# Stores on ScalarE's queue, and buffers moved from decays to rows and recalled tiles, in a hybrid attention and state-space layer

## The chip, the cores and the metric

The kernel runs on one core of a Trainium2 chip. The metric is the device time in microseconds (us) of one execution. The engines are TensorE (PE, with its weight loads PEld), VectorE (DVE), ScalarE (ACT), GpSimd (POOL) and SyncE (SP), whose queue issues DMAs.

## The reference

Four stages in a row change x, of 4 x 256 tokens with 512 features in float32: an attention, a gated feed-forward, a state-space mixer, and the feed-forward again. The change lies in the mixer. Cut to what matters:

```python
x = x + attention(layernorm(x))
x = x + ffn(layernorm(x))
x = x + mixer(layernorm(x))
x = x + ffn(layernorm(x))

def mixer(u):                       # H=128 heads of 64, G=8 groups, state 128
    gate, xBC, dt = split(u @ in_proj_w.T)
    hs, Bm, Cm = split(silu(causal_conv4(xBC) + conv_b))
    dt = softplus(dt + dt_bias); cum = cumsum(dt * A)
    # per head: y[i] = sum_{j<=i} (C_i . B_j) exp(cum_i - cum_j) dt_j x_j
    y = ssd(hs, ...) + D * hs
    g = y * silu(gate)
    g = g * rsqrt(mean(g*g over each of 8 groups) + eps) * norm_w
    return g @ out_w.T
```

The reference sums over chunks of 32 tokens and carries a state; the kernel forms the whole sum over 256 tokens per head directly, as a lower triangular matrix of decays times scores.

## The kernel before, in words

All matrix products that need float32 accuracy are made of three products of high and low parts (`mm3`, L115 to L117); `split` (L107, L108) makes the parts, the high one on ScalarE, the low one on VectorE or GpSimd.

The mixer runs over 64 blocks of 128 inner channels, 8 blocks to a group. One block i has two heads, 2i and 2i+1. It does the following:

- It projects its 128 channels of x (pp, 24 matmuls of 128x512) and convolves them: L964 on ScalarE, three taps at L971 on VectorE, SiLU at L975 on ScalarE. The result is x2, turned to token rows by trx (L1027) and scaled to xd (L1030).
- It projects the gate (again pp) and takes its SiLU, gt, on ScalarE (L1218).
- `differences` makes the decays em of each of the two heads from r, a row of cumulated values that `rows` (L996) loads from memory broadcast to all partitions. Four subtractions L1004 on VectorE, a mask L1008 on GpSimd, which overwrites half of r, then exponentials on ScalarE: four at L1013, one at L1014, four at L1016, the last readers of r.
- `weighted` (L1020) multiplies em by the scores gm of the group, on VectorE.
- `product` (L1044) multiplies em by xd on TensorE, for the block before. It is the last reader of em of both heads.
- `gated` adds the skip term (L1054), multiplies by gt (L1057) to gb, stores gb to the DRAM tile spill (L1059), squares it (L1064 for the first block of a group, L1066 for the others, which overwrites x2), and adds the squares up on GpSimd (L1067).

One group later the stored blocks come back: `recall` loads half a tile, gr (L1103), and splits it to gh; `partial` multiplies it by the output weights wo into pog, and `scaled` (L1115) adds it to x. `PER` says how many tiles of the group before are recalled in each block. In the first block of a group new scores are made. `fetch` (L811) loads the projection's weights wr, and `out_weights` (L1076) the output weights wor.

Who comes when: from block 8 on TensorE's order is that of the program text. The orders on the other engines and on SyncE's queue come from a planner that takes whatever its own estimate of time says is ready, the earlier in the text first. A queue runs its list strictly in order. `load` is `nc.sync.dma_start`, so in the mixer every transfer, loads and stores alike, stands in SyncE's one list. A tile with a tag has a number of buffers (`bufs`); a new tile waits until the oldest buffer's last reader is done. gh has three buffers, gb three, gt one.

The mixer's blocks are called in this order of steps:

```python
x2 = conv(projected("x", i, turn), i, "x2", 2)
...
inner_products(i - 1)
...
nc.scalar.activation(gt, pp, AF.Silu)
...
em.append(differences(h, rr.pop(h)))
if h + 2 < H:
    rr[h + 2] = rows(h + 2)
```

In the blocks 7, 0 and 1 of a group (from group 0's block 7 on) the inner products come between the two halves of the gate's projection, otherwise ahead of it. A row is thus always asked for two heads ahead.

Of the kernel before, what the change touches and what calls it, by code (L numbers as in the profile page):

```python
# [9 lines left out]
F32 = mybir.dt.float32  # L10
# [4 lines left out]
AF = mybir.ActivationFunctionType  # L15
# [5 lines left out]
P = 128  # L21
B, L, C = 4, 256, 512
NT = B * L
# [7 lines left out]
GB = NB // G  # L31
# [48 lines left out]
def hybrid_kernel(  # L80
# [6 lines left out]
    nc = tc.nc  # L87
    load = nc.sync.dma_start
# [16 lines left out]
    def split(hl, v, engine=nc.vector):  # L105

        nc.scalar.copy(hl[0], v)  # L107
        engine.tensor_tensor(hl[1], v, hl[0].bitcast(F32), ALU.subtract)  # L108
# [677 lines left out]
    def mixer(feed, later):  # L786
        with ExitStack() as es, ExitStack() as inner:
# [8 lines left out]
            po_ = pool("mo", 2, **freed)  # L796
# [52 lines left out]
            first = [ps_p.tile([P, NT], F32, name="pp", tag="pp") for _ in range(2)]  # L849
# [42 lines left out]
            p2 = inside("m2", 2, **freed)  # L892
# [99 lines left out]
                    yield  # L992

            def rows(h):
                r = p2.tile([P, NT], F32, name="r", tag="r", bufs=2)
                load(r, cumd[h : h + 1, :].to_broadcast([P, NT]))  # L996
                return r

            def differences(h, r):

                e = p2.tile([P, B, 3, P], F32, name="em", tag="em", bufs=4)
                rv = r.rearrange("p (b c i) -> p b c i", b=B, c=2)
                for b in range(B):
                    nc.vector.tensor_scalar(  # L1004
                        e[:, b, 2, :], rv[:, b, 1, :], col_t[:, h, b, 1:2], 0.0,
                        ALU.subtract, ALU.min,
                    )
                nc.gpsimd.affine_select(  # L1008
                    rv[:, :, 0, :], rv[:, :, 0, :], pattern=[[0, B], [1, P]],
                    compare_op=ALU.is_ge, fill=-1e30, base=0, channel_multiplier=-1,  # L1010
                )
                for b in range(B):
                    nc.scalar.activation(e[:, b, 1, :], rv[:, b, 1, :], AF.Exp, bias=col_t[:, h, b, 2:3])  # L1013
                nc.scalar.activation(e[:, :, 2, :], e[:, :, 2, :], AF.Exp)  # L1014
                for b in range(B):
                    nc.scalar.activation(e[:, b, 0, :], rv[:, b, 0, :], AF.Exp, bias=col_t[:, h, b, 0:1])  # L1016
                return e
# [33 lines left out]
            def gated(n, x2, gt, py, sq):  # L1051

                gb = po_.tile([P, NT], F32, name="gb", tag="gb", bufs=3)
                nc.vector.scalar_tensor_tensor(  # L1054
                    gb, x2, dh[:, n : n + 1], py.rearrange("p b t -> p (b t)"), ALU.mult, ALU.add
                )
                nc.vector.tensor_tensor(gb, gb, gt, ALU.mult)  # L1057
                if n < NB - 1:
                    load(spill[(n // GB) % 2][n % GB], gb)  # L1059
                else:  # L1060
                    last.append(gb)
                if sq is None:
                    sq = p2.tile([P, NT], F32, name="sq", tag="sq")
                    nc.scalar.activation(sq, gb, AF.Square)  # L1064
                else:
                    nc.scalar.activation(x2, gb, AF.Square)  # L1066
                    (nc.gpsimd if n < NB - 1 else nc.vector).tensor_tensor(sq, sq, x2, ALU.add)  # L1067
                return sq

            last = []  # L1070
            spill = [dram.tile([GB, P, NT], F32, name=f"spill{i}") for i in range(2)]
# [24 lines left out]

            def recall(g, t, half):

                r = po_.tile([P, 4, P], F32, name="gr", tag="gr", bufs=2)
                s = [po_.tile([P, 4, P], F32R, name=f"gh{j}", tag=f"gh{j}", bufs=3) for j in range(2)]  # L1100
                ts = slice(t * P, (t + 1) * P)
                n = 3 if half == 1 and g == G - 1 else 4
                load(r[:, :n, :], spill[g % 2][half * 4 : half * 4 + n, :, ts].rearrange("k p t -> p k t"))  # L1103
                split([v[:, :n, :] for v in s], r[:, :n, :])
                if n < 4:
                    split([v[:, n, :] for v in s], last[0][:, ts])
                return s
# [52 lines left out]
            def inner_products(m):  # L1160
                px2, gt, xd, em = stage.pop(m)
                py = product(xd, em)
                sqs[m // GB] = gated(m, px2, gt, py, sqs.get(m // GB))
# [5 lines left out]
            for _ in range(B):  # L1169
                next(scoring)  # L1170
            rr = {h: rows(h) for h in range(2)}
            stage, sqs, wos, rgs, todo = {}, {}, {}, {}, []
            recalled = []
            PER = {1: 1, 2: 2, 3: 1, 4: 1, 5: 2, 6: 1}
            def block(i, scoring, gm):
# [44 lines left out]
                for h in (2 * i, 2 * i + 1):  # L1220
                    with tc.issue_after(silus[2]) if i == 0 else ExitStack():
# [3 lines that stand above are left out]
# [6 lines left out]
                for _ in range(PER.get(gi + 1, 0)):  # L1231
                    if todo:
                        q, t = todo.pop(0)
                        recalled.append((q, t, [recall(q, t, half) for half in range(2)]))
# [19 lines left out]
            def begun(t):  # L1254
                pos[t] = ps_o.tile([P, C], F32, name="pog", tag="po")
                partial(pos[t], G - 1, recall(G - 1, t, 0), 0)
# [20 lines left out]
            for t in range(TT):  # L1277
                po = pos.pop(t)
                partial(po, G - 1, recall(G - 1, t, 1), 1)
                scaled(G - 1, t, po)  # L1280
                if t + 4 < TT:
                    begun(t + 4)
                feed.norm.stats(t)
                rooted = feed.norm.root(t, t + 1)

                with tc.issue_after(rooted) if t == TT - 1 else ExitStack():
                    for n in range(*{TT - 2: (0, 0), TT - 1: (t - 2, t)}.get(t, (max(0, t - 1), t))):
                        fed(n)
                xn = f2.tile([P, C], F32, name="gxn", tag="gxn")
                tr = ps.tile([P, KC, P], F32, name="tr", tag="m")  # L1290
                turned_[t] = [f2.tile([P, KC, P], F32R, name=f"gxs{j}", tag=f"gxs{j}", bufs=3) for j in range(2)]
                feed.norm.turned(t, xn, tr, turned_[t])
# [78 lines left out]
```

## Time and profile before

| | |
|---|---|
| median of 3 runs | 1880.39 us (1879.66 to 1881.84) |
| the profiled execution | 1881.98 us, its span 1880.2 us |
| attention and first feed-forward | 0 to about 408 us of the span |
| mixer's group 0, with nothing to recall | about 408 to 560 us |
| groups 1 to 7 | about 560 to 1785 us, some 180 us each |
| last recalls, second feed-forward, output | about 1785 to 1880 us |
| row load r, 512 KB at its destination, x128 | 3.9 us from issue to landing |
| store of gb, 512 KB, x63 | 3.0 us |
| recall gr, 256 KB, x120 | 3.0 us |

The span is that of the instructions from the first to the last; the execution's own time has a little around it. In the profile's busy tables each engine has its busy time in us, its share of the span, and the number of instructions. In the lists of waits each line reads: who waited, for whom, us in total, how many times, and in the queue's list the longest. The chain of waits gives start, duration and what. A busy TensorE need not be one at full speed; the pitch of its matmuls tells.

### The profile page before, as it was taken

To read this page: it belongs to the slowest core of one execution; us is meant where nothing else is said; L and a number is where in the kernel's file an instruction comes from. 1 tells how busy PE (TensorE), PEld (TensorE's weight loads), DVE (VectorE), ACT (ScalarE), POOL (GpSimd) and SP (SyncE) were. 2 spreads that over 40 slices of the span, in tenths; PEclk is the share of its full clock that TensorE was granted. 3 is DMA by queue.
4 is the path that set the end of the run, shared out by engine and by line. 5 is a ranking of instruction groups with operands and counts; after the bars stand their busy time and mean duration, and the time that the engine had idled before them with its cause. 6 is when DMAs were issued, how large, how long until landed. Compare 5 with 4: busy or idle time off the path is not lost.

```text
span 1880.2 us, 29875 instructions
## 1 busy us (share of the span) xinstructions
PE 1802.6 (96%) x10706; PEld 1449.8 (77%) x10706; DVE 1516.1 (81%) x2272; ACT 1467.9 (78%) x2886; POOL 452.0 (24%) x425
## 2 busy tenths in 40 slices
PE   8999988899999999999999999999999999999997
PEld 6777767677777887888788878877888888788876
DVE  5566667789999788977987898888888977897867
ACT  6666675379999788888888898888788978897653
POOL 6332230014441122112211311131222212321200
PEclk9999999899999999999999999999999999999999
DMA  4000000134465445544554455445535544554341
GB/s 144 1 1 1 22 15 16 34 101 157 166 199 187 133 151 164 179 140 135 196 163 140 146 176 166 143 138 184 164 128 169 184 150 131 185 175 151 101 125 50
DMA packets 152773, 240.35 MB, mean 128 GB/s; under 512 B 12464, under 2 KB 77616, under 8 KB 152624
## 3 DMA queue, kind: packets, MB, share of 16 engines
q1 hardware_dynamic: 152624, 238.44, 39.6%
q8 instruction: 84, 1.38, 0.3%
q14 instruction: 65, 0.53, 0.1%
HBM read 202.75 MB, written 35.65 MB: 127 GB/s over the span
## 4 chain that ended last, share of the span: by engine, by line
PE 59%; DVE 15%; ACT 14%; DMA 5%; issue 5%; POOL 1%; SPq 0%; ACTq 0%; DVEq 0%; POOLq 0%
PE pp L115 8%; PE pp L116 7%; PE pp L117 7%; PE pog L115 6%; PE pyy L1044 6%; PE pog L116 6%; PE pog L117 6%; DVE acc L971 4%; DVE em L1004 3%; DMA r<-cumd 3%; ACT e L477 2%; PE trx L1027 1%; ACT L1218 1%; ACT em L1016 1%; ACT em L1013 1%
## 5 line engine op out<-in xcount | busy, mean ns | idle before, releaser
L115 PE MATMUL pp<-mx,w 128*128 128x512 f32 (+1 forms) x1160 | 463.7, 400 | 13.4 <-ACT gt L1218 8.9
L117 PE MATMUL pp<-mx,w 128*128 128x512 f32 (+1 forms) x1160 | 451.8, 389 | 0.0
L116 PE MATMUL pp<-mx,w 128*128 128x512 f32 (+1 forms) x1160 | 451.7, 389 | 0.0
L971 DVE SCALAR_TENSOR_TENSOR acc<-pp,cw_s,acc 128x1012 f32<-128x1012 f32 (+2 forms) x240 | 304.8, 1270 | 56.5 <-ACT acc L964 54.5
L1020 DVE TENSOR_TENSOR em<-em,gm 128x1536 f32<-128x1536 f32 x128 | 248.1, 1948 | 39.6 <-ACT em L1016 39.5
L1008 POOL TENSOR_SCALAR_AFFINE_SELECT r<-r 128x512 f32<-128x512 f32 x128 | 121.5, 950 | 655.1 <-DMA r<-cumd 496.4
L115 PEld LDWEIGHTS pp<-mx,w 128*128 128x128 f32 x1160 | 218.4, 188 | 67.0 <-ACT gt L1218 12.4
L117 PEld LDWEIGHTS pp<-mx,w 128*128 128x128 f32 x1160 | 218.3, 188 | 46.3 <-issue 0.6
L116 PEld LDWEIGHTS pp<-mx,w 128*128 128x128 f32 x1160 | 218.6, 188 | 40.7 <-issue 0.6
L1067 POOL TENSOR_TENSOR sq<-sq,acc 128x1024 f32<-128x1024 f32 x55 | 144.7, 2632 | 334.7 <-ACT acc L1066 334.7
L1013 ACT ACTIVATE em<-r,col_t 128x128 f32<-128x128 f32 x512 | 170.0, 391 | 43.5 <-DMA r<-cumd 25.6
L115 PE MATMUL pog<-wo,gh 128*128 128x512 f32 x512 | 203.1, 397 | 0.9 <-DVE xd L1030 0.8
L1004 DVE TENSOR_SCALAR em<-r,col_t 128x128 f32<-128x128 f32 x512 | 180.3, 405 | 28.6 <-PE pyy L1044 15.0
L116 PE MATMUL pog<-wo,gh 128*128 128x512 f32 x512 | 199.6, 390 | 0.0
L117 PE MATMUL pog<-wo,gh 128*128 128x512 f32 x512 | 199.5, 390 | 0.0
L1044 PE MATMUL pyy<-em,xd 128*64 128x256 f32 (+1 forms) x2048 | 183.1, 329 | 1.3 <-DVE em L1020 0.9
L1044 PEld LDWEIGHTS pyy<-em,xd 128*64 128x64 f32 x2048 | 129.7, 137 | 59.9 <-issue 15.5
L1016 ACT ACTIVATE em<-r,col_t 128x128 f32<-128x128 f32 x512 | 167.9, 390 | 0.4
L975 ACT ACT_TABLE_LOAD x69 | 88.5, 1283 | 48.0 <-DVE acc L971 47.2
L477 ACT ACTIVATE e<-sc,nmx 128x256 f32<-128x256 f32 (+1 forms) x256 | 104.2, 442 | 21.0 <-DVE nmx L471 20.9
L108 DVE TENSOR_TENSOR gh<-gr,gh 128x512 fp32r<-128x512 f32 (+1 forms) x128 | 110.8, 874 | 7.8 <-ACT gh L107 7.3
L115 PEld LDWEIGHTS pog<-wo,gh 128*128 128x128 f32 x512 | 96.1, 188 | 26.0 <-issue 5.8
(290 smaller groups left out, 3306.9 us busy)
## 6 DMA issues: line engine op xcount, KB each, us to landing
wr<-in_win_dram SPq DMA_DIRECT2D x287, 256.0 KB, 2.7
r<-cumd SPq DMA_DIRECT2D x128, 512.0 KB, 3.9
spill<-gb SPq DMA_DIRECT2D x63, 512.0 KB, 3.0
gr<-spill SPq DMA_DIRECT2D x120, 256.0 KB, 3.0
wor<-in_wout_dram SPq DMA_DIRECT2D x64, 256.0 KB, 3.7
out_dram<-x SPq DMA_DIRECT2D x8, 256.0 KB, 2.3
x<-in_x_dram SPq DMA_DIRECT2D x1, 1536.0 KB, 8.7
gr<-spill SPq DMA_DIRECT2D x8, 192.0 KB, 2.5
```

Source lines behind the costliest of these rows:

```text
L115: nc.tensor.matmul(o, lh, rh, start=(first and k == 0), stop=False)
L116: nc.tensor.matmul(o, lh, rl, start=False, stop=False)
L117: nc.tensor.matmul(o, ll, rh, start=False, stop=(last and k == n - 1))
L477: nc.scalar.activation(es_[c][:, 2 * j + pr, :], sc[:, j, :], AF.Exp, bias=nm[:, j : j + 1], accum_out=rs[:, c, h : h + 1],)
L971: nc.vector.scalar_tensor_tensor(av[:, :, d:], pv[:, :, : L - d], cw_s[:, ch, tap : tap + 1], av[:, :, d:], ALU.mult, ALU.add,)
L1004: nc.vector.tensor_scalar(e[:, b, 2, :], rv[:, b, 1, :], col_t[:, h, b, 1:2], 0.0, ALU.subtract, ALU.min,)
L1008: nc.gpsimd.affine_select(rv[:, :, 0, :], rv[:, :, 0, :], pattern=[[0, B], [1, P]], compare_op=ALU.is_ge, fill=-1e30, base=0, channel_mult ...
L1013: nc.scalar.activation(e[:, b, 1, :], rv[:, b, 1, :], AF.Exp, bias=col_t[:, h, b, 2:3])
L1016: nc.scalar.activation(e[:, b, 0, :], rv[:, b, 0, :], AF.Exp, bias=col_t[:, h, b, 0:1])
L1020: nc.vector.tensor_tensor(e, e, gm, ALU.mult)
L1044: nc.tensor.matmul(py[d, b, k * P :], xd[:, 2 * b + k, d], es2[hh][:, b, 2 * k : 2 if k == 0 else 3, :].rearrange("p s i -> p (s i)"), sta ...
L1067: (nc.gpsimd if n < NB - 1 else nc.vector).tensor_tensor(sq, sq, x2, ALU.add)
```

## The change

The number of buffers of r and of gr goes from two to three, that of em from four to three. The store of a block is issued from ScalarE's queue in place of SyncE's, and stands behind the Square of the same block in the text. The Square itself and the sum of squares are the same as before, written in another order.

```diff
             def rows(h):
-                r = p2.tile([P, NT], F32, name="r", tag="r", bufs=2)
+                r = p2.tile([P, NT], F32, name="r", tag="r", bufs=3)
...
             def differences(h, r):
-                e = p2.tile([P, B, 3, P], F32, name="em", tag="em", bufs=4)
+                e = p2.tile([P, B, 3, P], F32, name="em", tag="em", bufs=3)
...
                 nc.vector.tensor_tensor(gb, gb, gt, ALU.mult)
+                first = sq is None
+                if first:
+                    sq = p2.tile([P, NT], F32, name="sq", tag="sq")
+                nc.scalar.activation(sq if first else x2, gb, AF.Square)
                 if n < NB - 1:
-                    load(spill[(n // GB) % 2][n % GB], gb)
+                    nc.scalar.dma_start(spill[(n // GB) % 2][n % GB], gb)
                 else:
                     last.append(gb)
-                if sq is None:
-                    sq = p2.tile([P, NT], F32, name="sq", tag="sq")
-                    nc.scalar.activation(sq, gb, AF.Square)
-                else:
-                    nc.scalar.activation(x2, gb, AF.Square)
+                if not first:
                     (nc.gpsimd if n < NB - 1 else nc.vector).tensor_tensor(sq, sq, x2, ALU.add)
...
             def recall(g, t, half):
-                r = po_.tile([P, 4, P], F32, name="gr", tag="gr", bufs=2)
+                r = po_.tile([P, 4, P], F32, name="gr", tag="gr", bufs=3)
```

## The prediction

> **What bounds the kernel now.** I read five views in this order: the busy table, the busy time by stage, TensorE's own waits, the chain of waits inside one group, and the waits of SyncE's DMA queue. The busy table and two stages (columns: start:end, length, then PE, PEld, DVE, ACT, POOL busy, each with its count):
>
> ```profile
> PE 1802.6 (96%) x10706; PEld 1449.8 (77%) x10706; DVE 1516.1 (81%) x2272; ACT 1467.9 (78%) x2886; POOL 452.0 (24%) x425
> ...
> 408.00:560.00 152.00, 145.26 (x822) 113.91 (x822) 142.39 (x177) 141.27 (x253) 64.77 (x42) 1.00 0.52 172
> ...
> 1060.00:1240.00 180.00, 177.90 (x978) 143.20 (x977) 153.06 (x194) 151.76 (x257) 38.48 (x27) 1.00 0.49 158
> ```
>
> See two regimes. In group 0 of the mixer (408 to 560 us) TensorE, VectorE and ScalarE are all above 92%. In groups 1 to 7 TensorE has 177.9 of 180 us. Busy matmuls could hide stretching, so I checked their pitch in the timeline: the 128x512 products start 0.227 us apart, for long stretches without a break. TensorE is the bound there, and all that can be won is its waits. Between 560 and 1785 us they are:
>
> ```profile
> PE pp L115 <- ACT gt L1218: 8.3, 5, 1.7
> PE trx L1027 <- ACT acc L975: 4.7, 5, 1.7
> PE pog L115 <- DVE xd L1030: 0.8, 1, 0.8
> PE pp L115 <- DVE acc L971: 0.7, 2, 0.4
> ```
>
> That is 14.5 us; 13.0 of it is ScalarE being late, once in a group. The chain of waits shows why (start, length, what):
>
> ```profile
> 1087.57 2.40 DMA wr<-in_win_dram
> 1089.98 0.33 SPq L811
> 1090.40 5.11 DMA r<-cumd
> 1095.90 0.68 ACT em L1013 x2
> 1096.60 1.28 ACT L975
> ...
> 1103.44 1.03 ACT gt L1218
> 1104.52 0.50 PE pp L115
> ```
>
> The row load of head 66 goes out at 1090.40, behind a weight fetch on SyncE; ScalarE stands still 4.3 us for it (exponentials, L1013), then runs the SiLUs late, and TensorE waits until gt at 1104.5. Such a load cannot be earlier, since its buffer is that of head 64, whose last reader (L1016) ends at 1088.5. SyncE's queue shows what else holds loads:
>
> ```profile
> SPq L1103 <- DVE gh L108: 191.4, 67, 8.3
> ...
> SPq L996 <- ACT em L1016: 160.2, 72, 5.2
> ...
> SPq L1059 <- DVE gb L1057: 113.3, 40, 11.7
> ```
>
> L1103 waits for a buffer of gr, L996 for one of r, L1059 for the block it is to store. One queue in order: behind each of them stand weight, row and recall loads.
>
> **What the Trainium skill says.** (1) "DMA: Bandwidth & Descriptors", section "Issuing engines are not separate DMA queues": issuing from several engines saves only the issuer's time, since all run on the same 16 engines. The trace agrees in size: a store costs SyncE 0.33 us and lands after 3.0. (2) "Advanced Engine Details and Errata", section "Sequencer Loop": compute instructions are queued ahead and the sequencer works on a control instruction meanwhile. So an issue on ScalarE can lie under the 1.05 us Square in front of it. Nothing in this trace shows it, ScalarE issues no DMA before. (3) "ScalarE: Activation LUTs", section "What ACT_TABLE_LOAD costs": 1283 ns for each change of set plus a drain of about 1380. The trace agrees on the 1283, and shows no drain: gt starts 1.29 us after its load does. (4) "Perfetto Trace Analysis", section "Optimization Strategy": the same gap repeating on the engine that should be full can mean too few buffers. It agrees: the gap before gt, up to 1.7 us by the waits, returns in five groups.
>
> **The change part by part.**
>
> Memory: per partition r gains 4 KB (1024 x 4 bytes), gr 2 KB, em loses 6 KB (4 x 3 x 128 x 4). Sum zero, nothing else has to move.
>
> *Rows, third buffer.* The load of head h needs the buffer of h-3 in place of h-2. For head 66 that is head 63, done with at 1074.7 in place of 1088.5: 13.8 us earlier, while the late landing cost 4.3. It covers that with 9 us to spare even if the fetch stays in front. I credit the two ScalarE waits of TensorE, 8.3 + 4.7 = **13.0 us**. Ends: nothing, if another wait takes the place (below), and 14.5 + 6.7 (TensorE idle in 408 to 560) + 2.1 (its wait for trx at 1786) = 23.3. GpSimd's 496 us wait for r is worth nothing: it is at 24%.
>
> *Recalled tiles, third buffer.* ScalarE's wait for gr's landing is 1.1 us in all; the 44.0 us it waits in front of gh (L107) are for TensorE to free gh, which keeps three buffers. The 191.4 us are SyncE's. Nothing by itself, covered by recalls running a block ahead. The 128 recall issues are the same in number; they and weight fetches may go earlier into DMA engines that are 50% busy. Between -2 and +2 us; I take 0.
>
> *The store.* Removed from SyncE: 63 issues x 0.33 = 20.8 us and waits of 113.3 us for gb, none on TensorE's path by the waits above. Added to ScalarE: the same 63 issues. It waits only for gb, which Square needs too (the DRAM slot is from two groups back), so behind it no new wait stands; queued after it are exponentials, SiLUs and casts. From below 0 (all under the Square's 1.05 us), from above 63 x 0.33 = 20.8 us of ScalarE. In groups 1 to 7 ScalarE is idle 28 of 180 us, which covers 8 x 0.33 = 2.6 per group; in group 0 it is at 93%, so I charge **2.6 us** there. The Squares (56 of 1.05, 8 of 1.04) keep their number. A block leaves some 1.1 us later if the store really goes behind the Square; gb has three buffers, and products start at least 13 us apart, so that is free.
>
> *Decays, one buffer fewer.* em for head h needs the buffer of h-3 in place of h-4. A block i uses heads 2i and 2i+1, and both go free when its product (L1044) ends. Even heads are not touched: 2i+4 waits for product i both ways, since 2i and 2i+1 are of one block. Odd head 2i+3 now waits for product i, not i-1. So from the end of product i to the start of product i+1 a whole odd head must be made: four L1004, nine exponentials (3.2 us on ScalarE plus a table load of 1.28), L1020 of 1.75. In the timeline of one group, odd heads start 22.5 to 4.1 us ahead of product i, so all shift. The room is 22.8 us in most blocks, but 14.7 before the product of block 6 of a group and 13.4 before that of block 7. Even heads do such a chain now, starting when the product ends: head 62 from 1057.9 to 1067.0, 9.1 us; head 58 from 1006.6 to 1026.9, 20.3. If odd heads take the first places after a product, 9.1 fits into 13.4, covered by matmuls; I charge 0 in groups 1 to 7. In group 0 there is less room: for blocks 0 to 7 the odd head starts ahead of the product by 1.5, 8.1, 0.8, 3.4, 3.8, 2.7, 1.1, 5.7 us, and its L1020 ends ahead of the next product by -2.7, -4.3, 2.9, 3.4, 5.0, 1.2, 7.4, -0.7. Lead beyond positive slack is 1.5 in block 5; in 0, 1 and 7 the head ends late because ScalarE is full, so a later start need not move its end. I charge **1.5 us**; upper end 1.5 + 8.1 + 1.5 + 5.7 = 16.8.
>
> Sum: -13.0 + 2.6 + 1.5 = -8.9 us. The profiled execution took 1881.98 us (span 1880.2 and 1.8 around it), 1.6 above the median 1880.39. So 1873.1 for such an execution, and **1871.5** for the median.
>
> **Rivals.**
>
> *No change: the odd head takes the place of the row wait.* At 1091.5, when product 31 ends, head 65 now comes due as well, with 3.2 us of exponentials, where ScalarE stood 4.3. Then SiLU and gt are only about 1.1 us earlier and most of the 13.0 stays: a quarter (3.3) less 2.6 gives 1879.7. For it: the same place in each group. Against: SiLU comes earlier in the block's order, and its input is ready at 1092.8.
>
> *Slower: odd heads miss their product.* Place: products of block 7 in a group, with 13.4 us of room. It decides when the chain of an odd head takes more than that; between 9.1 and 20.3 the middle is 14.7, that is 1.3 x 7 groups = 9 us, and group 0's 16.8 beside it. With the rows' gain kept and the store charged: -13.0 + 2.6 + 9 + 16.8 = +15.4, 1896; without the gain 1909. For it: TensorE has no other work in its fixed order, and ScalarE is busy nearly throughout 1060 to 1091. Against: these heads rank ahead of the next block's work.
>
> *It doesn't do what it says.* Orders on ScalarE, VectorE and SyncE come from a planner; new buffers can reshuffle them, and with them the table loads (52 for gt alone, 1.28 us each). One pair more per block is 64 x 2.6 = 164 us of ScalarE against some 200 idle in groups 1 to 7; that would show as SiLUs late everywhere. It goes either way and widens both cases.
>
> **How the numbers follow.** Forecast 0.48, no change 0.18, slower rival 0.34. A measurement can tell about 0.2%, 3.8 us. Half of reshuffling falls with the first and third. Faster 0.51 (forecast, and 0.03 of no change), within 0.2% 0.15, slower 0.34. The range goes from 1855 (the 23.3 us end, 1857, and 2 for spread) to 1902, between the 1896 and 1909 of the slower rival: left out are some 0.03 below and 0.15 above.
>
> **What would show it.** Right: ScalarE's wait for r (25.6 us) near zero, TensorE's waits for gt and acc below 4 us, stores on ScalarE with Squares unchanged, SyncE's wait at L1059 gone, and TensorE's wait for em (now about 1 us) still small. Wrong: TensorE waiting for L1020 before the product of a group's block 7 or in group 0, more than 240 table loads on the mixer's exponentials and SiLUs, or pp still waiting for gt.

## The result, and the profile after

| | median | runs |
|---|---|---|
| before, beside the changed kernel | 1884.54 us | 11 |
| the changed kernel | 1887.98 us | 11 |

The ratio is 1.0020, 95% interval 1.0008 to 1.0032: 2 to 6 us slower, where 8.9 us faster was forecast. The three runs of before shown ahead lie below the medians that later runs of it gave (1883.3 to 1884.8 us, single runs from 1875 to 1890), so a kernel is judged by its ratio to before's runs beside it. The profiled execution of the changed kernel has a span of 1887.9 us. In it the gate's SiLU has moved to L1219, the Square to L1061, the store to L1064, the recall to L1104.

The busy table and the two stages shown of before:

```profile
PE 1814.7 (96%) x10706; PEld 1459.8 (77%) x10706; DVE 1470.2 (78%) x2272; ACT 1456.8 (77%) x2876; POOL 465.8 (25%) x425
...
408.00:560.00 152.00, 144.78 (x805) 112.27 (x804) 130.79 (x166) 138.75 (x253) 62.28 (x41) 1.00 0.53 172
1060.00:1240.00 180.00, 178.75 (x983) 144.17 (x980) 146.44 (x194) 148.66 (x254) 39.31 (x27) 1.00 0.50 158
```

In a middle group TensorE is now busy 178.75 of 180 us, before 177.90: better. Group 0 has 144.78 of 152, before 145.26: no gain there. TensorE's waits from 560 to 1785 us, all that the answer has:

```profile
PE pg L986 <- DVE gm L991: 8.6, 7, 1.4
PE pyy L1044 <- DVE em L1020: 0.3, 1, 0.3
```

The waits for gt and for the SiLU of x2, 13.0 us, are gone, as forecast. A new one has come, once in a group as well: the scores' matmuls (pg) wait for VectorE to empty the earlier ones (gm). The chain of waits at the place shown of before:

```profile
1094.79 1.27 DVE acc L971
...
1096.64 1.27 DVE acc L971
1097.91 0.47 DVE gm L991
1098.43 0.70 PE pg L986 x2
```

No row load stands in it. VectorE comes late to the convolution's taps, and gm after them: measured from the start of product 31 (1091.4, before 1088.7), the first tap starts 1.6 us behind it (1093.0), before 0.6 ahead (1088.1), since ScalarE starts the convolution (L964) 0.4 ahead of it (1091.0), before 2.2 (1086.5). SyncE's queue answers to its lines of before:

```profile
SPq L1104 <- DVE gh L108: 241.8, 87, 7.5
SPq L996 <- ACT em L1016: 237.4, 76, 8.1
```

The wait for gb has left it, but the waits for buffers of gr and r have grown (191.4 and 160.2 before): loads are issued earlier, and then wait for the next buffer.

To see where the time went I divide each profiled span at the first matmul of a product (L1044) in the timeline: group 0 goes from the third masked copy of x (at 365 to 370 us in all profiles) to product 8, groups 1 to 7 on to product 63, the end from there. Table loads (`ACT_TABLE_LOAD`, 1.28 us each, which stand where ScalarE changes between exponentials and SiLUs) are counted beside them.

| profiled execution | group 0, us | its loads | groups 1 to 7, us | end, us | loads from product 8 to the last product's end | of these from product 56 on |
|---|---|---|---|---|---|---|
| before | 197.7 | 30 | 1225.9 | 90.1 | 219 | 22 |
| changed | 201.8 | 32 | 1220.5 | 96.6 | 207 | 28 |
| buffers alone (e2) | 195.0 | 26 | 1225.9 | 91.7 | 202 | 22 |
| em 3 alone (e3) | 202.8 | 32 | 1226.3 | 91.8 | 202 | 22 |
| store alone (e1) | 204.4 | 30 | 1233.6 | 90.1 | 226 | 25 |

The changed kernel loses 4.1 us in group 0 and 6.5 at the end, and wins 5.4 between. Of the 6.5, 2.2 us are a wait for em inside the last product, and 3.4 are two stretches in which TensorE ran at half its clock (last section). Single profiles spread: the same stretch of before's program (e9 below has its order on TensorE) differs by 4 us in groups 1 to 7, so sums of a few us are taken from the timed ratios, and the stretches say where.

### The profile page after: what moved, and what is told of

It is laid out like the page before. It is cut to its first block, busy times and chain, and to the rows that moved or that the text cites. A ratio compares the mean times of both kernels' runs of the same rounds, so it can differ in the third digit from the quotient of the medians.

```text
span 1887.9 us, 29843 instructions
## 1 busy us (share of the span) xinstructions
PE 1814.7 (96%) x10706; PEld 1459.8 (77%) x10706; DVE 1470.2 (78%) x2272; ACT 1456.8 (77%) x2876; POOL 465.8 (25%) x425
## 4 chain that ended last, share of the span: by engine, by line
PE 76%; ACT 9%; DVE 8%; issue 3%; POOL 2%; DMA 2%; SPq 0%; ACTq 0%; DVEq 0%; POOLq 0%
PE pp L115 12%; PE pp L116 12%; PE pp L117 11%; PE pyy L1044 9%; PE pog L115 6%; PE pog L116 6%; PE pog L117 6%; PE trx L1027 2%; ACT e L477 2%; DVE acc L971 2%; PE ptr L493 1%; PE pq L115 1%; PE pq L116 1%; PE pq L117 1%; DVE eT L494 1%
## 5 line engine op out<-in xcount | busy, mean ns | idle before, releaser
L1020 DVE TENSOR_TENSOR em<-em,gm 128x1536 f32<-128x1536 f32 x128 | 229.4, 1792 | 98.8 <-ACT em L1016 94.9
L1008 POOL TENSOR_SCALAR_AFFINE_SELECT r<-r 128x512 f32<-128x512 f32 x128 | 133.0, 1039 | 647.4 <-DMA r<-cumd 553.3
L1044 PE MATMUL pyy<-em,xd 128*64 128x256 f32 (+1 forms) x2048 | 191.4, 331 | 4.2 <-DVE em L1020 3.0
L1044 PEld LDWEIGHTS pyy<-em,xd 128*64 128x64 f32 x2048 | 135.8, 138 | 64.5 <-issue 20.9
L1004 DVE TENSOR_SCALAR em<-r,col_t 128x128 f32<-128x128 f32 x512 | 169.9, 386 | 14.3 <-PE pyy L1044 13.5
L1013 ACT ACTIVATE em<-r,col_t 128x128 f32<-128x128 f32 x512 | 167.3, 392 | 17.6 <-PE pyy L1044 15.1
L1016 ACT ACTIVATE em<-r,col_t 128x128 f32<-128x128 f32 x512 | 165.4, 388 | 0.3
L107 ACT CAST w<-wr 128x512 fp32r<-128x512 f32 x144 | 88.1, 612 | 69.5 <-PE pp L116 56.4
L1030 DVE TENSOR_TENSOR xd<-trx,dt_t 128x512 f32<-128x512 f32 x128 | 83.2, 683 | 64.9 <-PE trx L1027 64.8
L107 ACT CAST gh<-gr 128x512 fp32r<-128x512 f32 (+1 forms) x128 | 76.7, 605 | 58.4 <-PE pog L116 46.3
```

The source lines that it names most:

```text
L1004: nc.vector.tensor_scalar(e[:, b, 2, :], rv[:, b, 1, :], col_t[:, h, b, 1:2], 0.0, ALU.subtract, ALU.min,)
L1020: nc.vector.tensor_tensor(e, e, gm, ALU.mult)
L1044: nc.tensor.matmul(py[d, b, k * P :], xd[:, 2 * b + k, d], es2[hh][:, b, 2 * k : 2 if k == 0 else 3, :].rearrange("p s i -> p (s i)"), sta ...
```

## The experiments

All ratios are to the kernel before, timed on the same chip, with 95% intervals. The runs e1 to e4, e5 to e8 and e9 to e12 were timed on three chips, so a comparison between these sets is one of ratios.

**e1, the store alone.**

```diff
+                nc.scalar.activation(sq if first else x2, gb, AF.Square)
...
-                    load(spill[(n // GB) % 2][n % GB], gb)
...
+                    nc.scalar.dma_start(spill[(n // GB) % 2][n % GB], gb)
```

> The kernel before with one part of the change: blocks are stored from ScalarE's queue behind their Squares; r, gr and em keep 2, 2 and 4 buffers. Theory A (the loss of the change is the missing fourth buffer of em, above all at the last product, where nothing covers it): within 3 us of before, last product (block 63) some 2.8 us long, gt and trx waits of TensorE in groups 1 to 7 still about 13 us. Theory B (the loss is ScalarE's 63 issues of 0.33 us and what they delay): slower by 4 to 20 us, most of it in group 0.

Measured: 1.0059 (1.0042 to 1.0076), 11 us slower. Theory A, which held the store harmless, falls. Theory B's time came, but not all in group 0: 6.7 us there and 7.7 in groups 1 to 7. In this profile five stretches of 3.4 us ran at half the TensorE clock, some 1.7 us each: two in group 0, two in groups 1 to 7, one around the last product; before's has none between 375 and 1872 us. The rest of the 7.7 us are waits: TensorE's from 560 to 1785 us add up to 18.8 us, before 14.5, and most are in a line that before does not have, for VectorE to add a recalled product to x (L1115 before):

```profile
PE trx L1027 <- DVE x L1116: 11.6, 6, 2.9
```

In group 0 some 3.3 us are left beside the clock, with no more table loads than before (30): what makes them is open.

**e2, the buffers alone** (the changed kernel, store back on SyncE).

> The changed kernel with the store put back on SyncE's queue: only the buffers differ from before (r 3, gr 3, em 3). Theory A: like the changed kernel, 2 to 7 us above before, the last product again about 11 us from its first to its last matmul instead of 2.8, gt waits gone and waits of pg for gm in their place. Theory B: faster than before by about 9 us, since r's third buffer is kept and the store's cost is gone.

Measured: 0.9990 (0.9980 to 1.0000). Neither theory: not slower, as A said, and not 9 us faster. TensorE's waits from 560 to 1785 us:

```profile
PE pg L986 <- DVE gm L991: 5.3, 6, 0.9
PE pog L115 <- DVE xd L1030: 3.0, 5, 0.6
PE pp L115 <- ACT gt L1218: 2.0, 6, 0.3
PE pyy L1044 <- DVE em L1020: 0.7, 2, 0.4
```

11.0 us, where before had 14.5: the buffers exchange one set of waits for another, and groups 1 to 7 last 1225.9 us as before, within the spread. With e2 the store's cost in the changed kernel is its ratio against the changed one's, 1.0020 - 0.9990 = 0.3%, 6 us. A part of it can come by way of the clock, which the last section ties to TensorE's waits: the granted clock averages 0.9869 over the changed kernel's 11 runs and 0.9895 over the 22 of e2. The difference, 0.0026 of 1885 us, is at most 4.9 us, an estimate from these figures.

**e3, em at three buffers alone.**

```diff
-                e = p2.tile([P, B, 3, P], F32, name="em", tag="em", bufs=4)
+                e = p2.tile([P, B, 3, P], F32, name="em", tag="em", bufs=3)
```

> The kernel before with em at 3 buffers and nothing else changed (r 2, gr 2, store on SyncE). Theory A: slower than before by 8 to 15 us: some 8 at the last product, and in groups 1 to 7 either nothing or a few us more, since ScalarE's wait for r stays and the odd heads come later. Theory B: within 3 us of before. A third reading (r's third buffer pays for nothing, all of the gain in groups 1 to 7 comes from the other order that em's three buffers bring): the gt waits disappear here too, although r has two buffers.

Measured: 1.0039 (1.0024 to 1.0053), 7 us slower, at another place than theory A said: group 0 (202.8 us), hardly at the end (91.8). In groups 1 to 7 the third reading holds: TensorE's waits are those of e2 to within 0.5 us in each line, although r has two buffers. The order there comes from em, not from r.

**e4, the changed kernel with the last head apart.** The decays of head 127 lie in a row's and a weight fetch's buffer:

```diff
+                if h == H - 1:
+                    e01 = p2.tile([P, B, 2, P], F32, name="eml", tag="r", bufs=3)
+                    e2 = pw.tile([P, B, P], F32, name="emk", tag="wr", bufs=3)
```

> The changed kernel, but the decays of head 127 alone lie in two tiles of their own, in buffers that are idle by then (a row's and a weight fetch's), so they need not wait for product 62. Theory A: the last product is 2.8 to 4 us long again, 7 to 8 us less than the changed kernel, so 3 to 5 us below before; groups 0 to 7 otherwise unchanged. Theory B: as slow as the changed kernel, within 2 us.

Measured: 1.0009 (1.0000 to 1.0019). The last product is 2.8 us long again and the end 90.8 us, but the ratio falls by 0.11%, 2 us, and not by 7 to 8; the intervals of the two overlap. Theory A had taken the whole length of the last product for loss. In the changed kernel ten matmuls of a recall run in it, which are work, and TensorE waits there for em no longer than this:

```profile
PE pyy L1044 <- DVE em L1020: 2.2, 1, 2.2
```

What remained was why the store costs the changed kernel time at the end and in group 0, and not between. ScalarE's timeline in group 0, first with the buffers alone, then changed (start, length, what):

```profile
463.24 1.28 ACT L975 ACT_TABLE_LOAD   x1 [0.25 <-DVE acc L971]
...
465.50 1.04 ACT L1066 ACTIVATE acc<-gb 128x1024 f32<-128x1024 f32 x1
466.45 1.01 ACT L1218 ACTIVATE gt<-pp 128x1024 f32<-128x1024 f32 x1
```

```profile
465.70 1.28 ACT L975 ACT_TABLE_LOAD   x1 [0.27 <-DVE acc L971]
...
468.07 1.28 ACT L1016 ACT_TABLE_LOAD   x1
468.18 0.33 ACTq L1064 DMA_DIRECT2D spill<-gb  x1
...
469.67 1.05 ACT L1061 ACTIVATE acc<-gb 128x1024 f32<-128x1024 f32 x1
470.74 1.28 ACT L1219 ACT_TABLE_LOAD   x1
```

The store goes out at 468.18 while a table is being loaded, ahead of the Square that stands before it in the program text: its 0.33 us delay nothing. Of the 63 issues in this profile 57 lie from start to end under other work of ScalarE, table loads included, and the others leave 0.2 us in all uncovered. But the planner has put one exponential between the SiLU of x and that of the gate, and each such interruption costs two loads, 2.57 us. Theory C is: the store costs by the order that it brings, not by its issue.

**e5, extra table loads.** Store on SyncE, and in blocks 2, 4 and 6 one exponential of one column between the two SiLUs:

```diff
+EXTRA = (2, 4, 6)
...
+                if i in EXTRA:
+                    with tc.issue_after(silus[-1]):
+                        extra = nc.scalar.activation(
+                            stat.tile([P, 6], F32, name="primed", tag="st")[:, 0:1], ones[:, 0:1], AF.Exp
+                        ).ins
...
+                with tc.issue_after(extra) if extra is not None else ExitStack():
+                    nc.scalar.activation(gt, pp, AF.Silu)
```

> The buffers alone (store on SyncE), with one tiny exponential of one column put between the SiLU of x and the SiLU of the gate in blocks 2, 4 and 6: ScalarE's list then has 8 more table loads in group 0 (40 in place of 32 up to the eighth gate), 8 x 1.28 = 10.3 us, and no store. Its small result is not used. Theory C (what the store on ScalarE costs in group 0 is not its 0.33 us of issue but table loads: the planner puts exponentials between SiLUs, 32 loads in the changed kernel's group 0 against 26 with the buffers alone): group 0 becomes 6 to 11 us longer than with the buffers alone, like the changed kernel's, the rest unchanged. Theory B (the issue itself): no more than 1 to 2 us longer, since nothing is issued on ScalarE.

Measured: 1.0023 (1.0012 to 1.0034), 0.33% above the buffers alone, as much as the store costs. Group 0 lasts 200.7 us with 34 loads, against 195.0 with 26: 5.7 us for 10.3 us of loads. Table loads are enough to make a loss of about this size in group 0, with nothing issued on ScalarE.

**e6, the store from GpSimd's queue.**

```diff
-                    nc.scalar.dma_start(spill[(n // GB) % 2][n % GB], gb)
+                    nc.gpsimd.dma_start(spill[(n // GB) % 2][n % GB], gb)
```

> The changed kernel with the stores issued from GpSimd's queue in place of ScalarE's; buffers 3, 3, 3. ScalarE's list has 243 table loads against 262. Theory C: group 0 and the end lose most of what the changed kernel lost there (5 to 8 us and 3 to 5 us), and if the 5.4 us that it won in groups 1 to 7 come from a SyncE queue without stores, they stay: 1876 to 1882. If they come from ScalarE's order, they go: 1880 to 1885. Theory B: the same as with SyncE's store or better, 1876 to 1883, and table loads would not matter.

Measured: 0.9984 (0.9972 to 0.9996), 1881.7 us. Group 0 is back at 194.9 us with 28 loads; groups 1 to 7 have 1219.6, so the changed kernel's gain there stays. It fits a SyncE queue without stores as its cause; but ScalarE's list is another here too (192 loads against 207 from product 8 on), so that is not shown. The end, 94.5 us, is not better by 3 to 5. Here too the planner has an exponential and its two loads between the SiLUs of the last block, with no store on ScalarE, and TensorE waits 2.4 us for em inside the last product; a stretch at half the clock follows.

**e7, without gr's third buffer** (r 3, em 3, gr 2, store on SyncE).

> The buffers alone, without gr's third: r 3, em 3, gr 2, store on SyncE. If r's third buffer makes the 7.8 us between em 3 alone and all buffers in group 0 (where nothing is recalled), this is as fast as all buffers, within 2 us, group 0 at about 195 us from the first feed-forward's end. If gr's third does it, by way of the planner, it is as slow as em 3 alone (some 7 us above before).

Measured: 0.9992 (0.9981 to 1.0002), as all buffers; group 0 lasts 194.6 us. gr's third buffer brings nothing that can be told, and r's makes the 8 us in group 0 between e3 (202.8) and this run.

**e8, the buffers alone with the last head apart.**

> The buffers alone (store on SyncE), with the decays of head 127 in idle buffers of their own, as in the earlier run with the changed kernel. If em's missing buffer costs at the end what the trace of the buffers alone shows (last product and tail 91.7 us against 90.1 before), this gains 1 to 3 us over the buffers alone: 1879 to 1881, some 0.2% below before. If the end's loss came with the store, it gains nothing.

Measured: 0.9986 (0.9976 to 0.9996), 0.04% below e2. The intervals overlap, and the end (91.8 us) is as long as e2's, though with one stretch at half the clock, 1.7 us, that e2's has not: inconclusive.

**e9 and e10, r's third buffer with em's four.** A control has one buffer for sq, which frees 4 KB per partition; then r takes them (the last two lines below, in e10 alone).

```diff
-                    sq = p2.tile([P, NT], F32, name="sq", tag="sq")
+                    sq = p2.tile([P, NT], F32, name="sq", tag="sq", bufs=1)
...
-                r = p2.tile([P, NT], F32, name="r", tag="r", bufs=2)
+                r = p2.tile([P, NT], F32, name="r", tag="r", bufs=3)
```

> A control: the kernel before with one buffer for the sum of squares sq in place of two, which frees 4 KB per partition. Its 272 table loads are those of before. Expected within 2 us of before (sq is needed twice only when a group begins): then it can carry the next run. If it is slower, that cost is to be taken off the next run's.

> The control with r at three buffers and em kept at four (sq 1, gr 2, store on SyncE): r's third buffer by itself, which the prediction credited with 13.0 us in groups 1 to 7. If that step was right: ScalarE's wait for r near 0, TensorE's waits for gt and acc gone, 9 to 13 us below the control. If the gain is only there with em's three (the planner then orders the exponentials otherwise): ScalarE's waits for r go, but its list has 287 table loads against 272, and the time is within 4 us of the control or above it.

Measured: the control 0.9996 (0.9980 to 1.0012); with r's third buffer 0.9978 (0.9967 to 0.9989), the lowest ratio of all. It gains 2.8 us over the control by the medians, 3.4 by the ratios, not 9 to 13; the two intervals overlap. ScalarE's wait for r and TensorE's waits from 560 to 1785 us with it:

```profile
ACT L1013 <- DMA r<-cumd: 2.8, 1, 2.8
```

```profile
PE pp L115 <- ACT gt L1218: 7.4, 6, 1.2
PE pp L115 <- ACT em L1016: 0.9, 1, 0.9
```

The 25.6 us for which exponentials waited for rows are gone; the line that is left is one wait of a table load (2.2 us in before). TensorE's wait for the SiLU of x2 has gone from 4.7 us to nothing, yet that for gt is 7.4 us, before 8.3. But it is another wait. Before's stands behind products 15, 23, 31, 39 and 55, 1.6 to 1.7 us each, and none is left there: gt of block 32 now starts 9.0 us behind the start of product 31, before 14.7. So the row load did hold it there, as far as an edit that also reorders ScalarE can show. The new wait stands one block earlier, behind products 14, 22, 30, 38, 46 and 54, 1.2 us each. ScalarE and TensorE in block 31:

```profile
1084.65 1.28 ACT L1016 ACT_TABLE_LOAD   x1
1085.95 0.41 ACT L1016 ACTIVATE em<-r,col_t 128x128 f32<-128x128 f32 x1
...
1087.32 1.28 ACT L1218 ACT_TABLE_LOAD   x1
1088.62 1.02 ACT L1218 ACTIVATE gt<-pp 128x1024 f32<-128x1024 f32 x1
```

```profile
1089.69 0.50 PE L115 MATMUL pp<-mx,w 128*128 128x512 f32 x1 [1.23 <-ACT gt L1218]
```

In before and in the control no table is loaded between the two SiLUs of these six blocks; here two are, in each of the six. In sum TensorE's waits from 560 to 1785 us fall from the control's 11.4 us to 8.8, by 2.6 us, which is about what the times show.

**e11, extra loads where TensorE is the bound** (blocks 33 to 35 and 41 to 43).

> The buffers alone with the same tiny exponentials as in the earlier run of extra table loads, but in blocks 33 to 35 and 41 to 43, where TensorE is the bound: 6 more loads, 33 in place of 30 in each of the groups 4 and 5. Its small result is not used. If loads cost only where ScalarE is full (group 0, the end): within 1.5 us of the buffers alone in those groups. If every load counts: 7.7 us longer.

Measured: 1.0009 (0.9999 to 1.0019), 0.19% above e2's ratio, the intervals just touching. In the profile the two groups with 33 loads last 181.3 and 181.1 us, in e2 180.7 and 180.3: 1.4 us for 7.7 us of loads. By the profiles more than half of a load counts in group 0, here about a fifth; by the ratios alone, 3.6 us, it could be up to half.

**e12, GpSimd's store and the last head apart together.**

> What the runs point to together: buffers 3, 3, 3, stores from GpSimd's queue, and head 127's decays in idle buffers. 242 table loads. With GpSimd's store 0.16% below before and the last head apart worth some 1.5 us with the buffers alone, 1877 to 1881, that is 2 to 6 us below before; if the end's gain does not add up here, as with GpSimd's store alone, 1881 to 1883.

Measured: 0.9982 (0.9971 to 0.9994), 1879.75 us. Below both kernels, and not to be told from GpSimd's store alone.

**All profiles side by side.** In 13 of the 14 profiles group 0 lasts the longer the more tables ScalarE loads in it, within some us; e5, whose loads were put in by hand, stands apart: 193.5 to 195.0 us with 26 loads (e2, e7, e8, e11), 194.9 and 198.0 with 28 (e6, e12), 197.7 to 204.4 with 30 (before, e9, e10, e1), 201.4 to 202.8 with 32 (e4, changed, e3), 200.7 with 34 (e5). The longest, e1, has the two stretches at half the clock; e10 and e12 have one each.

## Why the prediction was wrong, point by point

**What bounds the kernel: right for groups 1 to 7.** No variant won more there than TensorE's waits hold. But the outcome was decided outside them: in group 0, which lasts 193.5 to 204.4 us in the variants, and at the last product.

**Rows, 13.0 us: the step that failed most.** It credited the whole of TensorE's waits for gt and x2 to the row load, and took no other wait in their place, though it named that as the lower end. The waits did go, and others came. With r's buffer alone (e10) the 13.0 us become 7.4 us for gt one block earlier, behind two more table loads, and the term is 2.6 us by the waits and 2.8 to 3.4 by the times. With em's three buffers r's third does another thing: it repairs group 0, where em alone costs (8 us between e3 and e7), and does nothing in groups 1 to 7. In the changed kernel TensorE's waits there fall from 14.5 to 8.9 us, and the span by 5.4. The rival that an odd head takes the place of the row wait describes those groups well: in the changed kernel the exponentials of heads 64 and 65 run from 1092.6 on, where ScalarE had stood for the row of head 66 (head 63's L1020 ended at 1091.2, 0.2 us ahead of product 31), and pg's wait of up to 1.4 us has come for gt's of up to 1.7.

**Recalled tiles, 0: right.** e7 is as fast as e2.

**The store, 2.6 us: the wrong cause and under half of the size.** The issue is 0.33 us, as read, and lies under other work, as the Trainium skill lets expect ("Advanced Engine Details and Errata", section "Sequencer Loop": engine instructions can be read and queued while the sequencer executes a control instruction); the trace now shows it, at 468.18. The cost, 6 us, goes with the order: 32 loads against 26 in group 0 (+6.8 us) and 28 against 22 around the last products (+4.9 us, of which 3.4 are the two stretches at half the clock), with 5.4 us won between. That loads suffice for the part in group 0 is shown by e5; that they make all of it is not, since e1 loses time there with no load more. The third rival had named the planner and the loads, but not which way it would go, and its sign, more than 240 loads on the mixer's exponentials and SiLUs, did not come: before has 240 and the changed kernel 230. Not their number had grown, but their number in group 0 and at the end. "ScalarE: Activation LUTs", section "What ACT_TABLE_LOAD costs", has the 1283 ns that each load takes here; the drain of about 1380 that it adds again does not show, the gate's SiLU starts 1.29 us after the start of its load.

**Decays, 1.5 us: the place was incomplete.** By themselves the three buffers cost 7 us (e3), 5.1 of it in group 0, inside the range that the prediction gave them there (1.5 to 16.8). What it never looked at is block 63. Between two products a block's projections give room; after product 62 only half a projection and a turn of x2 are left. In before's profile 6.5 us pass there to the last product's start, less than the 9.1 us that the prediction took for a head's chain. Before, head 127 was ready at 1782.6; the changed kernel begins it when product 62 ends, at 1784.8. ScalarE then works like this:

```profile
1789.09 1.28 ACT L1016 ACT_TABLE_LOAD   x1
1790.39 0.40 ACT L1016 ACTIVATE em<-r,col_t 128x128 f32<-128x128 f32 x1
...
1791.76 1.28 ACT L1219 ACT_TABLE_LOAD   x1
...
1794.09 1.28 ACT L1014 ACT_TABLE_LOAD   x1
1795.39 0.63 ACT L1014 ACTIVATE em<-em 128x512 f32<-128x512 f32 x1
```

Three loads until one head's remaining exponentials are done, the middle one for gt, which stands between them; L1020 ends at 1798.1, and the last product runs from 1791.3 to 1802.6, with the recall's matmuls, the wait of 2.2 us and the two stretches at half the clock in it. With the buffers alone one load stands there and L1020 ends at 1794.5. So the slower rival was right in kind (an odd head misses its product), wrong in place: not block 7 of each group, with its 13.4 us, but the one block that has no work behind it. e4 puts it at some 2 us, not clear of the noise.

**The sum.** In place of -13.0 + 2.6 + 1.5 the runs have -0.1% for the buffers together (e2, -2 us) and +0.3% for the store on top (6 us), the measured +0.2%. Of the numbers that were to show it right, the waits for r, gt and L1059 did go; that showed the step made, not the gain.

## What to carry to other kernels

A wait in the chain ahead of a late operation is its price only if nothing else would hold the operation next; take the wait away alone before crediting it, and look where the next one stands. Where a planner orders an engine that must load tables to change functions, count the table loads of the new order by stage, and not only in all: here an issue of 0.33 us cost nothing itself, and each pair of loads that came with it 2.57 us of a full ScalarE. When a buffer is given up, check its last use separately, where no further work covers a wait; and look whether waits bunch, since in these runs TensorE's clock fell behind bunched ones.

## What the runs showed of the hardware

TensorE's clock fell to half for stretches of 3.4 us. The two in the changed kernel's last product, each with the 3.4 us ahead of it (start:end, length, busy times, granted clock, DMA share, GB/s):

```profile
1788.40:1791.80 3.40, 1.62 (x10) 1.05 (x10) 3.40 (x8) 3.35 (x5) 0.00 (x0) 1.00 0.57 198
1791.80:1795.20 3.40, 3.40 (x9) 2.66 (x9) 0.02 (x1) 3.37 (x3) 2.37 (x1) 0.50 0.78 245
1795.20:1798.60 3.40, 1.20 (x9) 0.70 (x9) 2.26 (x2) 2.32 (x5) 0.15 (x1) 1.00 0.00 0
1798.60:1802.00 3.40, 3.40 (x24) 2.88 (x21) 0.82 (x2) 0.00 (x0) 0.00 (x0) 0.50 0.47 158
```

TensorE loses 1.7 us in each: in the first the 128x512 products start 0.43 us apart in place of 0.23. The 14 profiles have 16 such stretches between 380 and 1865 us, five of them in e1. In each profile they all start a whole number of steps of 3.41 us apart, and in the step just ahead of each one TensorE ran no matmul for 1.82 to 2.71 us. Of the 6058 other such steps at full clock one is as empty (1.84 us, e5), the next 1.72. So here, with that one exception, a stretch followed whenever waits emptied more than about half of one step, and such waits cost up to 1.7 us more than they last; a wait that fell across two steps, as before's of 2.1 us that ends at 1788.6, went without. The two stretches in the changed kernel's end depend on where the steps fall, which may be why e4 gave back less time than the profile promised.
